# Column copies in larger groups, a table in the order of lanes, and SP clearing the sums: a graph layer on one core

## The chip, the cores and the metric

The kernel runs on one core of a Trainium2 chip. The metric is the time of the program on the device in microseconds. Times of runs are given as the median of several; a profile is one execution, taken by the hardware profiler. The core has five engines with instruction queues of their own: TensorE (PE, with its weight loads listed as PEld), VectorE (DVE), ScalarE (ACT), GpSimd (POOL) and SyncE (SP). In the profile a name such as DVEq or SPq stands for the queue's own work: loading registers, waiting, issuing transfers.

## The reference

`x` holds 12500 nodes of 48 numbers; 400000 edges have a source `src`, a destination `dst` (sorted) and 32 attributes. Cut to what matters:

```python
h = maximum(layernorm(x), 0)                      # 12500 x 48
tmp = concatenate([h[dst], h[src], edge_attr], axis=1)   # 400000 x 128
hid = relu(tmp @ W1 + b1)                         # 400000 x 128
msg = hid @ W2 + b2                               # 400000 x 48
x = x + segment_sum(msg, dst, num_segments=12500)
```

## The kernel before

**Tables.** `h @ W1` is not computed per edge. `node_tables` normalizes the nodes and writes two tables to HBM, with 128 numbers for each node: `tab_a` (destination part with the bias) and `tab_b` (source part). The source table is also made a second time on chip, in `bt`, turned: 128 partitions hold the 128 hidden numbers, and each node is one column. `turn(i)` makes 1024 columns of it: four matmuls into PSUM and a copy by ACT (line 307). Node number `p * 98 + r` belongs to lane `p`, and column `n` of `bt` is node `n`, so the copy writes each lane's numbers 98 columns apart. Thirteen turns are spread over the first five iterations, `TURNS = 3` each.

**Chunks.** The main loop in `windows` runs over 391 chunks of 8 tiles of 128 edges (and two more iterations to drain). Its order is written out by hand (`tc.manual_schedule()`); each engine executes its own share in that order. For a chunk `c`:
- SP issues the loads of the edge attributes (`lhs`), of the destination numbers (`row`) and of the 80 rows of `tab_a` at the chunk's window (`rhs`), line 354 to 364. The window's address is a register: line 361 loads it together with the 15 node numbers of this chunk's row transfers.
- DVE makes the one-hot matrix of the window (`lhs`, line 379), and the compared `hot` (line 389).
- PE multiplies both parts (`before`, line 400), adds the source part (`gathered`, line 421), ACT applies the ReLU (`hidden`, line 437), and PE sums over edges by the one-hot matrix (`fold`, line 445, 448) into `p_g`. DVE adds `p_g` to the running sums of the window (`add`, line 460) two iterations later.

**The source part comes three ways.** Of the 8 tiles in a chunk, most are gathered from `tab_b` by POOL, one indirect transfer of 128 rows each (line 371) into one of seven buffers `gb`. About one tile in eight chunks is collected by SP, one transfer per row (`rows`, line 289, 15 per chunk). And about 1.1 tiles per chunk are collected from the turned table `bt` on chip by `columns`: one copy per edge, of one column of 128 numbers, from an address in a register (line 348). `PARTS` lists the groups of these copies: engine (True is DVE), place in the strip of addresses, count. For each group the queue loads its addresses from SBUF into registers (`numbers`, line 272) and then copies. In an iteration DVE has groups of 8, 15, 16, 20 and 12 (71 copies) and ACT groups of 12, 8, 8, 20, 12 and 12 (72 copies), 143 together; a load takes a whole number of fours, and in the group of 15 the 16th register is the place of the sum (`PLACE`).

**Segments.** Sums are kept for 1024 nodes at a time in one of two buffers `segs`, for 12 chunks (`GQ`), `k` counting them. At `k = 11` `segment_next` clears the other buffer by two memsets on DVE (line 476) and carries 80 columns over. In the next segment PE multiplies the old sums by `W2` at `k = 0` and `1` (`segment_sum`, line 488, 489), DVE adds the result to `x` (`segment_add`, line 495), and at `k = 2` SP stores it (line 499).

An `If` on a flag chooses between `windows` and a general path, which doesn't run with these inputs.

Of the kernel before, what the change touches and what calls it, by code (L numbers as in the profile page):

```python
# [8 lines left out]
F32 = mybir.dt.float32  # L9
# [42 lines left out]
TURNS = 3  # L52
BLOCKS = (NPAD + CE - 1) // CE
BUILD = (BLOCKS + TURNS - 1) // TURNS
COLS = BUILD
# [10 lines left out]
STRIP = 144  # L66
# [3 lines left out]
RPART = 15  # L70
BASE = 0

BT0 = 16512
SEG0 = 161696
# [3 lines left out]
AT_PLACE, AT_SEG, SEG, NEXT = 16, 17, 18, 19  # L78
WIDTH = 20
# [13 lines left out]
EPS = 1e-5  # L93

# [135 lines left out]
def windows(nc, tc, gp, bt, ident, idx, raw, rhss, x_t, tab_a, tab_b, dst, edge_t, w2s, b2s,  # L230
            sources, out_t):
# [4 lines left out]
    with ExitStack() as es:  # L236
# [24 lines left out]
        gss = {}  # L261

# [31 lines left out]
        bt_v = bt.rearrange("h (p r) -> h r p", r=NR)  # L294

        def turn(i):

            n = min(T, NR - i * T)
            p_t = ps_p.tile([P, T, HID], F32, name="pre")
            parts = p_t.rearrange("h (k q) p -> h k q p", k=2)  # L300
            for k in range(2):
                nc.tensor.matmul(
                    parts[:, k, : n // 2, :].rearrange("h q p -> h (q p)"), wb[:, k, :],
                    ht[: 2 * D, i * T // 2 : (i * T + n) // 2, :].rearrange("k g p -> k (g p)"),
                    start=True, stop=True,
                )
            nc.scalar.copy(
                bt_v[:, i * T : i * T + n, :].rearrange("h (q k) p -> h q k p", k=2),
                parts[:, :, : n // 2, :].rearrange("h k q p -> h q k p"),
            )  # L310
# [14 lines left out]
        def columns(c, part):  # L325

            dve, at, n = PARTS[part]
            first = (c - COLS) * PART + FIRST_OF[part]
            n = max(0, min(n, len(BYCOLS) * P - first)) if c >= COLS else 0
            engine = mybir.EngineType.DVE if dve else mybir.EngineType.Activation  # L330
            copy = nc.vector.tensor_copy if dve else nc.scalar.copy
            place = PLACE if at < PLACE <= at + PARTS[part][2] and c >= 2 else None
            size = -(-n // 4) * 4 if place is None else place + 1 - at
            if not n:
                if place is not None:
                    st[c - 2]["base"], = numbers(c, place, 1, engine, cols)
                return
            got = numbers(c, at, size, engine, cols)
            if place is not None:
                st[c - 2]["base"] = got[place - at]  # L340
            for k, of in enumerate(got[:n]):
                j, e = divmod(first + k, P)
                if j not in gts:
                    gts[j] = gtc.tile([HID, P], F32, name="gt")
                of = of.with_bounds(
                    min_val=BT0, max_val=BT0 + 4 * (N - 1), guaranteed_mod_val=0, out_of_modulus=4
                ) - BT0
                copy(gts[j][:, e : e + 1], bt8[:, bass.ds(of, 4)].bitcast(F32))  # L348

        def prepare(c):  # L350
# [10 lines left out]
            base, *nodes = numbers(c, BASE, 1 + m, mybir.EngineType.SP)  # L361
# [109 lines left out]
        def segment_next(g):  # L471

            old, new = segs[g % 2], segs[(g + 1) % 2]
            if g > 0:
                for k in range(2):
                    nc.vector.memset(new[:, k, W:], 0.0)  # L476
# [24 lines left out]
        with tc.manual_schedule():  # L501
            for c in range(NCH + 2):
# [9 lines left out]
                columns(c, 1)  # L512
# [35 lines left out]
                for i in range(c * TURNS, min((c + 1) * TURNS, BLOCKS)):  # L548
                    turn(i)
# [130 lines left out]
def tile_gnn_preln(  # L680
# [15 lines left out]
    ones: bass.AP,  # L696
    w1: bass.AP,
# [52 lines left out]
    with tc.tile_pool(name="keep", bufs=1) as keep, tc.tile_pool(  # L750
# [69 lines left out]
        def check():  # L820
# [10 lines left out]
            nc.vector.tensor_scalar(cols, cols, 4, BT0, op0=ALU.mult, op1=ALU.add)  # L831
            rows_at = slice(BASE, BASE + 1 + RPART)
# [7 lines left out]
            at = last[:, :, AT_PLACE : AT_PLACE + 1]  # L840
            nc.vector.scalar_tensor_tensor(
                at, last[:, :, AT_SEG : AT_SEG + 1], -4.0, at, op0=ALU.mult, op1=ALU.add
            )
            at_place = slice(PLACE, PLACE + 1)
            nc.vector.scalar_tensor_tensor(
                cols[:, :, at_place], cols[:, :, at_place], 1.0, at, op0=ALU.mult, op1=ALU.add
            )

# [5 lines left out]
    with tc.If(outside == 0) as cmp:  # L854
        windows(nc, tc, gp, bt, ident, (srci, rel, bw, wrow, last, cols, degs), (xg, wb, ht), rhss,
                x_t, tab_a, tab_b, dst16, edge_t, w2s, b2s, sources, out_t)
# [78 lines left out]
```

## Time and profile before

| | us |
|---|---|
| median of 3 runs (lowest, highest) | 3365.4 (3362.7, 3370.7) |
| the profiled execution | 3372.65 |
| its span | 3370.8 |
| DVE, ACT, POOL, PE busy | 2800, 3036, 2530, 2776 |

A row of grouped instructions reads: line, engine, operation, output <- inputs, shapes, count | busy time in us, mean of one in ns | idle time of the engine just before them, and what ended most of it. Copies are pipelined, so the mean of one (144 ns on DVE) is longer than their pace. "issue" is idle time in which the engine waited for nothing that the profile shows. In a timeline a row gives start and duration in us, and neighbouring instructions of one kind are merged (x15). A row of waits gives who waited, for whom, total us, times, longest.

### The profile page before, as it was taken

Reading aid. Unit: us, or ns where it says so; the run is one execution under the profiler, and the core shown is the slowest. Engines: PE = TensorE matmul, PEld = TensorE weight load, DVE = VectorE, ACT = ScalarE, POOL = GpSimd, SP = SyncE. Lnnn points to the kernel's source line nnn. Section 1 sums busy time; section 2 is a strip of 40 time slices with the busy share of each in tenths; the row PEclk is TensorE's granted clock in tenths of the full one; section 3 lists DMA queues with packets and bytes.
Section 4 is the critical chain, followed back from the end, with each engine's and each line's share of the span. In section 5 each row is a group of like instructions: output and inputs, shape, how many; then the busy total and the mean of one; then the engine's idle time right before and its main releaser. Section 6 shows DMA issues by size and latency. Waiting matters only on the chain.

```text
span 3370.8 us, 115212 instructions
## 1 busy us (share of the span) xinstructions
PE 2775.6 (82%) x16394; PEld 2158.3 (64%) x16394; DVE 2800.1 (83%) x29140; ACT 3035.6 (90%) x28179; POOL 2530.0 (75%) x2670
## 2 busy tenths in 40 slices
PE   7987778888888888888887788888788788788777
PEld 6666666666666666666666666676666666666565
DVE  6588888888888888888888888888888888888876
ACT  5799998999998999998899999889998999999987
POOL 7677777777777777777777777777777777777776
PEclk9999998998898998988889999888998999899989
DMA  7433333333333333333333333333333333333333
GB/s 262 122 97 104 100 97 100 99 101 100 100 99 100 95 100 102 100 101 97 100 98 101 100 100 102 95 101 97 102 99 98 97 100 98 104 100 97 99 96 83
DMA packets 200234, 349.24 MB, mean 104 GB/s; under 512 B 69219, under 2 KB 107749, under 8 KB 198181
## 3 DMA queue, kind: packets, MB, share of 16 engines
q0 software_dynamic: 84800, 172.53, 18.9%
q1 hardware_dynamic: 114258, 169.09, 16.7%
q14 instruction: 634, 5.19, 0.5%
q8 instruction: 138, 2.26, 0.3%
q10 hardware_dynamic: 404, 0.17, 0.0%
HBM read 322.05 MB, written 22.07 MB: 102 GB/s over the span
## 4 chain that ended last, share of the span: by engine, by line
DVE 71%; issue 14%; PE 5%; DVEq 4%; POOL 2%; DMA 2%; ACT 0%; SPq 0%; POOLq 0%; ACTq 0%
DVE gt L348 47%; DVE lhs L379 12%; DVE hot L389 8%; DVEq L272 4%; DVE seg L460 2%; POOL gb L371 2%; PE pre L400 1%; PE p_g L445 1%; DVE xseg L495 1%; DVE seg L476 1%; DMA row<-in_dst 1%; PE p_f L488 1%; PE p_f L489 1%; DMA gb<-tab_b,srci 1%; PE p_n L195 1%
## 5 line engine op out<-in xcount | busy, mean ns | idle before, releaser
L371 POOL DMA_INDIRECT gb<-tab_b,srci x2618 | 2489.4, 951 | 812.7 <-issue 724.4
L348 ACT COPY gt<-bt 128x1 f32 x27705 | 2618.0, 188 | 63.9 <-issue 54.6
L348 DVE COPY gt<-bt 128x1 f32 x27335 | 1842.1, 144 | 463.3 <-issue 435.1
L400 PEld LDWEIGHTS pre<-rhs,lhs 112*128 112x128 f32 x6250 | 823.5, 208 | 277.1 <-issue 193.4
L400 PE MATMUL pre<-rhs,lhs 112*128 112x128 f32 x6250 | 841.5, 292 | 98.3 <-issue 56.7
L445 PE MATMUL p_g<-hot,hid 128*128 128x80 f32 x6250 | 794.0, 282 | 131.2 <-ACT hid L437 129.1
L445 PEld LDWEIGHTS p_g<-hot,hid 128*128 128x128 f32 x6250 | 758.4, 198 | 164.4 <-ACT hid L437 161.6
L421 PE MATMUL pre<-gb,ident 128*128 128x512 f32 (+2 forms) x1548 | 771.2, 627 | 34.3 <-DMA gb<-tab_b,srci 26.5
L437 ACT ACTIVATE hid<-pre 128x1024 f32<-128x1024 f32 x391 | 397.5, 1017 | 220.2 <-PE pre L421 205.8
L379 DVE TENSOR_SCALAR_CACHE_REDUCE lhs<-row,bw 80x1024 f32<-80x1024 int16 x391 | 494.6, 1265 | 14.8 <-DMA row<-in_dst 14.5
L421 PEld LDWEIGHTS pre<-gb,ident 128*128 128x128 f32 x1548 | 311.8, 225 | 281.0 <-issue 261.7
L421 PE MATMUL pre<-ident,gt 128*128 128x128 f32 x860 | 214.9, 336 | 261.7 <-DVE gt L348 234.7
L421 PEld LDWEIGHTS pre<-ident,gt 128*128 128x128 f32 x860 | 143.8, 210 | 291.5 <-issue 136.4
L389 DVE TENSOR_TENSOR hot<-wnum,rel 128x640 f32<-128x640 f32 x391 | 318.2, 814 | 0.0
L460 DVE TENSOR_TENSOR seg<-seg,p_g 128x160 f32 x391 | 121.5, 311 | 47.8 <-PE p_g L448 47.8
L448 PE MATMUL p_g<-ident,deg 80*128 80x80 f32 x782 | 156.4, 283 | 0.0
L448 PEld LDWEIGHTS p_g<-ident,deg 80*128 80x128 f32 x782 | 123.6, 198 | 0.0
L488 PE MATMUL p_f<-seg,w2s 128*48 128x512 f32 (+1 forms) x134 | 82.2, 700 | 44.3 <-DVE xseg L495 43.9
L489 PE MATMUL p_f<-seg,b2s 1*48 1x512 f32 (+1 forms) x134 | 76.2, 650 | 0.0
L488 PEld LDWEIGHTS p_f<-seg,w2s 128*48 128x48 f32 x134 | 12.3, 135 | 85.9 <-DVE xseg L495 60.0
L476 DVE MEMSET seg<- 128x944 f32 x64 | 54.1, 845 | 9.3
L489 PEld LDWEIGHTS p_f<-seg,b2s 1*48 1x48 f32 x134 | 11.3, 122 | 65.2 <-issue 65.2
(76 smaller groups left out, 429.0 us busy)
## 6 DMA issues: line engine op xcount, KB each, us to landing
gs<-tab_b SPq DMA_DIRECT2D x5760, 0.5 KB
row<-in_dst SPq DMA_DIRECT2D x390, 160.0 KB
lhs<-in_edge_t SPq DMA_DIRECT2D x390, 128.0 KB
gb<-tab_b,srci POOLq DMA_INDIRECT x2618
rhs<-tab_a SPq DMA_DIRECT2D x391, 40.0 KB
xseg<-in_x_t SPq DMA_DIRECT2D x33, 192.0 KB
out_x<-xseg SPq DMA_DIRECT2D x33, 192.0 KB
tab_b<-tab SPq DMA_DIRECT2D x3, 1280.0 KB
```

Of the source, the lines that this page charges most:

```text
L272: return nc.values_load_multi_w_load_instructions(table[c % P : c % P + 1, c // P, at : at + n], engines=[engine], min_val=0, max_val=1 << 23,
L348: copy(gts[j][:, e : e + 1], bt8[:, bass.ds(of, 4)].bitcast(F32))
L371: nc.gpsimd.indirect_dma_start(out=gb[:, t, :], out_offset=None, in_=tab_b[:, :], in_offset=bass.IndirectOffsetOnAxis(ap=srci[:, c * T + t ...
L379: nc.vector.tensor_scalar(lhs[:W, : n * P], row[:, : n * P], bw[:, c : c + 1], None, op0=ALU.is_equal, op1=ALU.add, accum_out=deg[:, :1],)
L389: nc.vector.tensor_tensor(hot[:, :n, :], wnum.unsqueeze(1).to_broadcast([P, n, W]), rel[:, c * T : c * T + n].unsqueeze(2).to_broadcast([P ...
L400: nc.tensor.matmul(pre[:, t, :], s["lhs"][:K, t * P : (t + 1) * P], s["rhs"][:K, :], start=t % BANK == 0, stop=False, skip_group_check=True,)
L421: nc.tensor.matmul(pre[:, t:e, :], lhsT, rhs, start=False, stop=True, skip_group_check=True)
L437: nc.scalar.activation(h[:, :n, :], s["pre"][:, :n, :], AF.Relu)
L445: nc.tensor.matmul(p_g[:, 0, :], s["h"][:, t, :], s["hot"][:, t, :], start=t == 0, stop=t == n - 1)
L448: nc.tensor.matmul(p_g[:, 1, :], s["deg"], ident[:W, :W], start=True, stop=True)
L460: nc.vector.tensor_add(to, to, s["p_g"])
L488: nc.tensor.matmul(p_f[:, :n], w2s, seg[:, 0, s], start=True, stop=False)
```

## The change

- `bt` is written in the order of lanes: node `p * 98 + r` becomes column `r * 128 + p`, so a turn's copy writes runs of 128 columns. The 13 turns go to six iterations, as 2, 2, 2, 2, 3, 2, and the column copies begin at chunk 6 instead of 5.
- The addresses of columns are worked out on chip from node numbers, by a few more passes of DVE over the strips before the loop.
- 148 columns per chunk instead of 143: DVE in groups of 23, 16, 17, 16 (with the sum's place as the 24th register of the first), ACT in groups of 12, 16, 20, 12, 16. Two of ACT's groups stand before the activation and three behind it, as 28 and 44 copies before and 28 and 48 after.
- 16 rows per chunk by SP instead of 15; SP loads the node numbers of two chunks at once (32 registers), and the windows' addresses of eight chunks at once.
- The memsets of a segment's sums go; SP writes zeros from HBM over them in eight pieces, one per iteration from `k = 2` to `9` of the following segment.

```diff
-TURNS = 3
...
+TURNS = (2, 2, 2, 2, 3, 2)
+COLS = len(TURNS)
...
 PARTS = (
-    (True, 0, 8), (True, 8, 15), (True, 24, 16), (True, 40, 20), (True, 60, 12),
-    (False, 72, 12), (False, 84, 8), (False, 92, 8), (False, 100, 20), (False, 120, 12),
-    (False, 132, 12),
+    (True, 0, 23), (True, 24, 16), (True, 40, 17), (True, 60, 16),
+    (False, 76, 12), (False, 88, 16), (False, 104, 20), (False, 124, 12), (False, 136, 16),
 )
...
-RPART = 15
-BASE = 0
+RPART = 16
+BASE, BASES = 2 * RPART, 8
+CLEAR = 8
...
             nc.scalar.copy(
-                bt_v[:, i * T : i * T + n, :].rearrange("h (q k) p -> h q k p", k=2),
+                bt[:, i * CE : i * CE + n * P].rearrange("h (q k p) -> h q k p", k=2, p=P),
                 parts[:, :, : n // 2, :].rearrange("h k q p -> h q k p"),
             )
...
-            base, *nodes = numbers(c, BASE, 1 + m, mybir.EngineType.SP)
+            if c % BASES == 0:
+                bases[:] = numbers(c, BASE, BASES, mybir.EngineType.SP)
+            if c % 2 == 0 and c + 1 >= ROWS0:
+                ahead[:] = numbers(c, 0, 2 * RPART, mybir.EngineType.SP)
+            base, nodes = bases[c % BASES], ahead[c % 2 * RPART :][:m]
...
         def segment_next(g):
             old, new = segs[g % 2], segs[(g + 1) % 2]
-            if g > 0:
-                for k in range(2):
-                    nc.vector.memset(new[:, k, W:], 0.0)
...
+        def segment_clear(g, k):
+
+            n = 2 * (L - W) // CLEAR
+            half, at = divmod(k, CLEAR // 2)
+            nc.sync.dma_start(
+                segs[g % 2][:, half, W + at * n : W + (at + 1) * n],
+                zeros.unsqueeze(0).to_broadcast([P, n]),
+            )
...
                 columns(c, 0)
-                columns(c, 1)
                 segment_add()
                 if 0 <= c - 2 < NCH:
                     add(c - 2)
                     if k == GQ - 1:
                         segment_next(g)
-                columns(c, 2)
+                columns(c, 1)
                 if c < NCH:
                     compare(c)
...
+                columns(c, 2)
                 columns(c, 3)
                 columns(c, 4)
                 columns(c, 5)
-                columns(c, 6)
-                columns(c, 7)
                 if 0 <= c - 1 < NCH:
                     gathered(c - 1)
                     hidden(c - 1)
+                columns(c, 6)
+                columns(c, 7)
                 columns(c, 8)
-                columns(c, 9)
-                columns(c, 10)
...
+                if g > 0 and begin(g + 1) < NCH and 0 <= k - STORE < CLEAR:
+                    segment_clear(g - 1, k - STORE)
...
+            nc.vector.tensor_scalar(
+                at, cols, 1.0 / NR, 0.5 / NR - 0.5, op0=ALU.mult, op1=ALU.add
+            )
+            nc.vector.tensor_scalar_add(at, at, ROUND)
+
+            nc.vector.tensor_scalar(
+                at, at, -ROUND, 4.0 - 4.0 * NR * P, op0=ALU.add, op1=ALU.mult
+            )
+            nc.vector.tensor_scalar_add(at, at, float(BT0))
+
             nc.vector.scalar_tensor_tensor(
-                cols[:, :, at_place], cols[:, :, at_place], 1.0, at, op0=ALU.mult, op1=ALU.add
-            )
+                cols, cols, 4.0 * P, at, op0=ALU.mult, op1=ALU.add
+            )
```

More of the change, by code (lines that the diff above doesn't have):

```diff
@@ L93 @@
 EPS = 1e-5
+ROUND = 1.5 * 2**23
 G = 5
@@ L261, in windows @@
         gss = {}
+        bases, ahead = [], []
         def group(c):
@@ L547, in windows @@
                     sources()
-                for i in range(c * TURNS, min((c + 1) * TURNS, BLOCKS)):
-                    turn(i)
+                if c < COLS:
+                    for i in range(sum(TURNS[:c]), sum(TURNS[: c + 1])):
+                        turn(i)
                 if c < PIECES:
@@ L696, in tile_gnn_preln @@
     ones: bass.AP,
+    zeros: bass.AP,
     w1: bass.AP,
@@ L883 @@
     numbers[2 : NCH + 2, AT_PLACE] = SEG0 + of % 2 * SEG_SIZE - BT0
-    numbers[:NCH, BASE] = first
+    bases = np.pad(first, (0, -NCH % BASES)).reshape(-1, BASES)
+    numbers[: len(bases) * BASES : BASES, BASE : BASE + BASES] = bases
     numbers[:NCH, SEG] = seg
```

38 lines of the change are left out of this document (20 added, 18 removed).

## The prediction

> **What bounds the kernel now.** I read the page first (shares, chain), then the timeline of one engine over one iteration, then the waits of each engine between 130 and 3340 us, where 383 of the 391 chunks run.
>
> ```profile
> span 3370.8 us, 115212 instructions
> PE 2775.6 (82%) x16394; PEld 2158.3 (64%) x16394; DVE 2800.1 (83%) x29140; ACT 3035.6 (90%) x28179; POOL 2530.0 (75%) x2670
> ...
> DVE 71%; issue 14%; PE 5%; DVEq 4%; POOL 2%; DMA 2%; ACT 0%; SPq 0%; POOLq 0%; ACTq 0%
> ...
> L371 POOL DMA_INDIRECT gb<-tab_b,srci x2618 | 2489.4, 951 | 812.7 <-issue 724.4
> ```
>
> ACT has the highest busy share, yet the chain that ended last is DVE's, with 14% "issue": DVE waiting for nothing that the profile shows. The timeline of DVE in one iteration says what this is:
>
> ```profile
> 1509.83 1.28 DVE L379 TENSOR_SCALAR_CACHE_REDUCE lhs<-row,bw 80x1024 f32<-80x1024 int16 x1
> ...
> 1511.04 0.57 DVE L348 COPY gt<-bt 128x1 f32 x8
> 1512.02 1.00 DVE L348 COPY gt<-bt 128x1 f32 x15 [0.42 <-issue]
> 1512.94 0.31 DVE L460 TENSOR_TENSOR seg<-seg,p_g 128x160 f32 x1
> 1513.78 1.06 DVE L348 COPY gt<-bt 128x1 f32 x16 [0.52 <-issue]
> 1514.76 0.81 DVE L389 TENSOR_TENSOR hot<-wnum,rel 128x640 f32<-128x640 f32 x1
> 1515.76 1.30 DVE L348 COPY gt<-bt 128x1 f32 x20 [0.19 <-issue]
> 1517.30 0.82 DVE L348 COPY gt<-bt 128x1 f32 x12 [0.24 <-issue]
> 1518.04 1.26 DVE L379 TENSOR_SCALAR_CACHE_REDUCE lhs<-row,bw 80x1024 f32<-80x1024 int16 x1
> ```
>
> A gap stands before nearly every group of copies, where DVE's queue is loading the group's addresses into registers (line 272). One load of each size, from the view of that line in windows that hold one load (8, 12, 16, 20 registers), and the 31 loads of a single register:
>
> ```profile
> L272 DVEq TENSOR_LOAD <-cols x1: 607/607/607, 1501.7 to 1501.7; - x1
> ...
> L272 DVEq TENSOR_LOAD <-cols x1: 853/853/853, 1508.1 to 1508.1; - x1
> ...
> L272 DVEq TENSOR_LOAD <-cols x1: 1107/1107/1107, 1504.3 to 1504.3; - x1
> ...
> L272 DVEq TENSOR_LOAD <-cols x1: 1351/1351/1351, 1506.0 to 1506.0; - x1
> ...
> L272 DVEq TENSOR_LOAD <-last x31: 303/314/545, 224.9 to 3239.6; - x31
> ```
>
> (1351 - 607) / 12 = 62 ns per register, and 607 - 8 x 62 = 111 ns beside them. The five loads (8, 16, 16, 20, 12) take 607 + 2 x 1107 + 1351 + 853 = 5025 ns of an iteration of 1518.04 - 1509.83 = 8.21 us; the other 3.2 us hand out 71 copies and a few large operations, at most 43 ns each. So it is DVE's queue, not its datapath, that is full. It hardly waits for others:
>
> ```profile
> DVE gt L348 <- issue: 432.8, 1267, 1.2
> DVE seg L460 <- PE p_g L448: 21.0, 10, 3.4
> ...
> 130.00:3340.00 3210.00, 2644.51 (x15768) 2061.72 (x15767) 2717.82 (x28896) 2954.66 (x27991) 2429.21 (x2556) 0.91 0.36 99
> ```
>
> The rows are the waits and the window's busy times (PE, PEld, DVE, ACT, POOL). 21 us in 3210 is all that PE costs DVE. POOL is as full: 951 + 724.4 us / 2374 gaps = 1.256 us per gather, and 2618 of them are 3288 us. What it waits for, and its one long stall:
>
> ```profile
> POOL gb L371 <- PE pre L421: 16.4, 50, 1.5
> ...
> 127.82 0.95 POOL L371 DMA_INDIRECT gb<-tab_b,srci  x1 [12.98 <-PE pre L421]
> ```
>
> So DVE's queue and POOL run at nearly the same pace, and neither can gain much alone.
>
> **The change, part by part.**
>
> *DVE's groups.* With 148 column copies per chunk from chunk 6, there are (390-6) x 148 / 128 = 444 column tiles (430 before) and 48 row tiles (45). DVE does 72 copies per iteration for 71, in groups of 23, 16, 17, 16 for 8, 15, 16, 20, 12. Loads go up to whole fours, and the first takes the sum's place along: 24, 16, 20, 16 registers for 8, 16, 16, 20, 12. What differs is one load of 24 for one of 8 and one of 12: 111 + 24 x 62 = 1599 ns for 607 + 853 = 1460, **+139 ns** in 384 iterations: **+53 us**. No row has a load of 24; the line through four rows is taken, as the row of 20 is nearest to it. The ends are -20 us (if all of the single register's 303 ns were fixed cost, 303 - 111 = 192 ns more fall away with the load: -53 ns) and +98 us (if 24 cost what 8 and 16 do, 1714 ns: +254 ns). The 72nd copy costs at most 43 ns of the queue, and one load fewer to turn to gives about as much back: 0, ends -17 and +17 us. The datapath's part, 72 x 61 ns, lies under the queue.
>
> Here a page speaks the other way. The Trainium skill, page "DMA: Bandwidth & Descriptors", section "Latency and other measured facts", puts a floor of about 600 ns under a tensor load. By that, one load fewer would take up to 0.6 us off each iteration, 230 us in all, and POOL would set the end. The rows of one register (303 ns) contradict it here; the case it makes stands among the rivals.
>
> *Sums cleared by SP, not DVE.* At a segment's end DVE cleared 2 x 944 columns:
>
> ```profile
> 1526.28 1.27 DVE L379 TENSOR_SCALAR_CACHE_REDUCE lhs<-row,bw 80x1024 f32<-80x1024 int16 x1
> ...
> 1529.05 0.31 DVE L460 TENSOR_TENSOR seg<-seg,p_g 128x160 f32 x1
> 1529.51 1.84 DVE L476 MEMSET seg<- 128x944 f32 x2
> ...
> 1532.32 0.81 DVE L389 TENSOR_TENSOR hot<-wnum,rel 128x640 f32<-128x640 f32 x1
> ...
> 1535.53 1.27 DVE L379 TENSOR_SCALAR_CACHE_REDUCE lhs<-row,bw 80x1024 f32<-80x1024 int16 x1
> ```
>
> From sum to compare it is 3.27 us here and 1.82 us in the iteration above, but this iteration is only 9.25 - 8.24 = 1.0 us longer than the one before it, as the loads run under the clearing; 0.31 us of that (load of one register) and the 0.18 us copy stay. So 0.5 us x 31 = **-16 us**, not the 57 us that the memsets are busy; ends 0 (work only leaves DVE) and -45 (1.45 us x 31). DVE's waits for p_g come from the segment sums on PE, which stay, but PE gets more time per iteration: **-8 us** of 21 (ends 0, -21).
>
> *SP.* Its queue does about one iteration in 7.5 us:
>
> ```profile
> 1534.46 0.33 SPq L354 DMA_DIRECT2D lhs<-in_edge_t  x1
> ...
> 1537.03 4.81 SPq L289 DMA_DIRECT2D gs<-tab_b  x15
> 1541.95 0.33 SPq L354 DMA_DIRECT2D lhs<-in_edge_t  x1
> ...
> SPq L499 <- DVE seg L460: 153.4, 24, 12.0
> SPq L499 <- DVE xseg L495: 50.7, 8, 9.2
> ...
> L272 SPq TENSOR_LOAD <-last x449: 274/1187/1317, 134.7 to 3331.4; - x150
> ...
> 8.94 0.46 SPq L770 DMA_DIRECT2D last<-in_src_last  x1
> 9.44 0.93 SPq L771 DMA_DIRECT2D cols<-in_src_strip  x1
> ```
>
> One load of 32 registers per two chunks, at (1187 - 274) / 15 = 61 ns each, is 2.17 us for 2 x 1.19, and eight bases every eight chunks take 0.70 us back: nothing in sum, but even chunks come 1 us later and odd ones earlier. The 16th row DMA adds 4.81 / 15 = 0.32 us. The 256 clearing DMAs (8 x 32 segments) go to 128 partitions, as the last two rows do: 0.46 us taken, end 0.93. Per segment that is 12 x 0.32 + 8 x 0.46 = 7.5 us, against the 204 / 32 = 6.4 us that SP now stands waiting at the store (line 499). Queued behind each clearing DMA are the next chunk's edges, indices and window rows, for which DVE's compare and PE wait. The first of them waits for PE's last sum over that segment, which is done by then: the store just ahead of it has waited for DVE to add that sum. DVE writes to the cleared segment two iterations after the last piece is issued, so it finds it landed. SP's spare time is used up, and a little shows: **+6 us**, ends 0 and +39 (0.32 x 391 + 0.46 x 256 - 204).
>
> *ACT.*
>
> ```profile
> L348 ACT COPY gt<-bt 128x1 f32 x27608 | 2608.8, 188 | 63.3 <-issue 54.0 <-ACT gt L348 1.0
> L437 ACT ACTIVATE hid<-pre 128x1024 f32<-128x1024 f32 x383 | 389.7, 1017 | 192.1 <-PE pre L421 190.8 <-ACT gt L348 0.3
> ```
>
> (Both rows are of the window, not the page.) ACT's copies go from 72 to 76 per iteration, 1479 more at 94.5 ns (2608.8 us / 27608), +140 us, in groups of 12, 16 before the activation and 20, 12, 16 behind it. They fit into 192 + 63 us of idle time: 0, end +20 (no gain is possible, as work is only added).
>
> *POOL.* 2601 gathers for 2618: -17 x 1.256 = -21 us of its own time, all of it turned into waiting, as DVE is slower: 0.
>
> *Start.* Four iterations have two turns where they had three, and the last two have three and two in place of one and none; the node numbers' conversion adds four passes over 608 columns to DVE.
>
> ```profile
> L307 ACT COPY bt<-pre 128x1024 f32<-128x1024 f32 (+1 forms) x13 | 25.0, 1988 | 3.5 <-PE pre L302 3.5
> ...
> 44.11 0.45 DVE L831 TENSOR_SCALAR cols<-cols 128x576 int32<-128x576 int32 x1
> ```
>
> A turn's copy wrote with steps of 98 numbers; in the order of lanes it writes runs of 128, as `hid` does in 1017 ns (above): 13 x 0.97 = 12.6 us less on ACT. Columns start one iteration later, and the conversion costs 4 x 0.45 = 1.8 us. **+1 us**, ends -12 and +12.
>
> Sum: 53 + 0 - 16 - 8 + 6 + 0 + 0 + 1 = **+36 us**. The profiled run took 3372.65 us (span 3370.8, the rest around it), 7 us over the median of the three runs, 3365.4; against that median, 3365 + 36 = **3401 us**, +1.1%.
>
> **The rivals.**
> - *POOL decides, the load is mostly fixed cost* (faster). If a load of 24 takes no longer than those of 8 and 12 together (1460 ns), DVE's time falls by 16 + 8 us and more, and the end follows POOL: 3365 - 21 to 3365 - 21 - 16 (its waits for PE), about **3340**. For it: POOL's 1.256 us cadence hardly breaks. Against: the four loads lie on one line, 246, 254 and 244 ns per four registers.
> - *SP falls behind* (slower still). It decides once a clearing DMA's issue costs over 0.46 us: halfway to 0.93 it is 0.23 x 256 = 59 us on top of SP's +39: up to 3463; about **3440**. For it: spare 6.4 against 7.5 us per segment. Against: a slower DVE gives SP time too.
> - *ACT becomes the bound.* 76 x 94.5 + 1017 = 8.2 us per iteration, under 8.3; only if waits for PE stay as they are, 3365 + 140 - 63 = **3442**. In the Trainium skill, page "Perfetto Trace Analysis", section "Identifying the Most-Contended Engine", the engine of highest occupancy is the bound, which here is ACT, and adding to it would cost the full 140 us: 3505. Its 190.8 us of waits for PE say that it is not.
> - *Nothing comes of it*: the load's increase and what DVE loses cancel (53 - 45 - 8 = 0): **3365**.
>
> **How the numbers follow.** Sum as forecast (3375 to 3425) 0.55; SP 0.15; ACT 0.08; POOL 0.15; nothing 0.07. What a measurement of this kernel can tell from no change is about 0.2%, 7 us. So faster 0.15, same 0.07, slower 0.78. From half of POOL's case to most of SP's: 3345 to 3445.
>
> **What the changed profile would show.** The load of 24 near 1.6 us in DVE's queue, four loads per iteration, iterations near 8.35 us; POOL's waits for PE grown from 16 to some 70 us; ACT's waits for `pre` down to about 80 us; SP's waits at the store near zero, and no more than a few us of DVE waiting for `row`. The prediction is wrong if the load of 24 takes under 1.46 us, if POOL still runs without waits at a shorter total, or if DVE waits for `row` by tens of us.

## The result: 7% slower, and SP late

The changed kernel takes 3606.7 us (median of four runs, 3603.6 to 3614.2) against 3367.3 us for the kernel before beside it: a ratio of 1.0715 (95% interval 1.0692 to 1.0739). The forecast was 3401 us. The sign was right; some 205 us are missing from the sum. The profiled execution took 3609.8 us.

The page of the changed kernel: span, busy shares, the chain that ended last by engine, and two groups of instructions.

```profile
span 3608.0 us, 117497 instructions
...
PE 2891.0 (80%) x16428; PEld 2244.8 (62%) x16428; DVE 2782.5 (77%) x29394; ACT 3222.8 (89%) x29658; POOL 2494.4 (69%) x2653
...
DVE 27%; SPq 24%; DMA 15%; PE 14%; issue 11%; ACT 5%; DVEq 2%; POOL 1%; ACTq 0%; POOLq 0%
...
L373 POOL DMA_INDIRECT gb<-tab_b,srci x2601 | 2454.0, 943 | 1036.5 <-issue 733.5
...
L381 DVE TENSOR_SCALAR_CACHE_REDUCE lhs<-row,bw 80x1024 f32<-80x1024 int16 x391 | 495.8, 1268 | 117.4 <-DMA row<-in_dst 115.3
```

DVE's share of the chain fell from 71% to 27%. In its place stand SP's queue (24%) and transfers (15%), neither of which was over 2% before. All engines lost busy share. So much of the chain now waits for what SP issues. (ACT is still the busiest, at 89%, and has 5% of the chain. The Trainium skill, page "Perfetto Trace Analysis", section "Identifying the Most-Contended Engine", would name it as the bound; this chain does not.)

The waits of the engines, between 130 and 3580 us of the changed kernel:

```profile
POOL gb L373 <- PE pre L423: 259.0, 134, 7.5
...
ACT hid L439 <- PE pre L423: 168.8, 114, 6.3
...
DVE lhs L381 <- DMA row<-in_dst: 102.0, 126, 2.2
...
DVE seg L462 <- PE p_g L450: 18.8, 11, 2.9
```

One row of the same view of the kernel before, for comparison with the third:

```profile
DVE lhs L379 <- DMA row<-in_dst: 2.1, 5, 0.9
```

SP's queue in the changed kernel, same window. Line 289 issues the 16 row transfers; line 507 is the store at a segment's end:

```profile
SPq L289 <- DMA seg<-in_zeros: 58.8, 89, 1.7
SPq L289 <- DMA lhs<-in_edge_t: 57.7, 102, 1.5
SPq L507 <- DVE seg L462: 46.4, 23, 6.1
SPq L289 <- DMA row<-in_dst: 35.9, 102, 1.6
SPq L507 <- DVE xseg L503: 9.3, 7, 2.0
```

And before:

```profile
SPq L289 <- DMA row<-in_dst: 2.5, 7, 0.5
...
SPq L289 <- DMA lhs<-in_edge_t: 1.0, 4, 0.5
```

Two things are to be seen. First, SP itself is held up: its row transfers wait 152 us (58.8 + 57.7 + 35.9) for earlier transfers to land, where they waited 3.5 us for `lhs` and `row` before. The operands in the trace say how: each of SP's transfers signals one of eight semaphores in turn, and first waits until the transfer eight places earlier, which had the same one, has landed. (In the timeline below, the clear at 2013.82 us and the row at 2018.30 both have semaphore 102; that row starts 1.35 us after the row ahead of it, where 0.32 us is usual.) Second, `row` is late for DVE in 126 chunks, and yet SP still stands 56 us at the store.

The register loads came out as forecast. One load each of 24, 16 and 20 registers, from windows that hold one load:

```profile
L272 DVEq TENSOR_LOAD <-cols x1: 1598/1598/1598, 1529.6 to 1529.6; - x1
...
L272 DVEq TENSOR_LOAD <-cols x1: 1096/1096/1096, 1553.7 to 1553.7; - x1
...
L272 DVEq TENSOR_LOAD <-cols x1: 1351/1351/1351, 1551.7 to 1551.7; - x1
```

SP's timeline over one segment of the changed kernel shows what a clear does to it:

```profile
2004.63 0.37 SPq L485 DMA_DIRECT2D seg<-in_zeros  x1
2005.09 0.38 SPq L352 DMA_DIRECT2D lhs<-in_edge_t  x1
...
2008.64 5.13 SPq L289 DMA_DIRECT2D gs<-tab_b  x16
2013.82 0.36 SPq L485 DMA_DIRECT2D seg<-in_zeros  x1
2014.29 0.36 SPq L352 DMA_DIRECT2D lhs<-in_edge_t  x1
...
2015.95 6.44 SPq L289 DMA_DIRECT2D gs<-tab_b  x16
2022.45 0.36 SPq L485 DMA_DIRECT2D seg<-in_zeros  x1
2022.92 0.37 SPq L352 DMA_DIRECT2D lhs<-in_edge_t  x1
...
2069.57 0.33 SPq L352 DMA_DIRECT2D lhs<-in_edge_t  x1
...
2085.67 0.33 SPq L352 DMA_DIRECT2D lhs<-in_edge_t  x1
...
2096.47 5.16 SPq L289 DMA_DIRECT2D gs<-tab_b  x16
2104.41 0.34 SPq L507 DMA_DIRECT2D out_x<-xseg  x1
```

Two chunks with clears take 2022.92 - 2005.09 = 17.8 us of SP; two without take 2085.67 - 2069.57 = 16.1 us. Of the 1.7 us, 0.9 us are the two issues (2004.63 to 2005.09: 0.46 us each). The rest is mostly waiting: the 16 rows take 5.13 us in the chunk where a register load stands between `row` and `rhs`, and 6.44 us in the next one, where nothing does and the rows come round to the clear's semaphore before it has landed. At the end SP is done with its rows at 2101.63 and stands 2.8 us until the store can go.

### The profile page after: what moved, and what is told of

It is laid out like the page before. It is cut to its first block, busy times and chain, and to the rows that moved or that the text cites. A ratio compares the mean times of both kernels' runs of the same rounds, so it can differ in the third digit from the quotient of the medians.

```text
span 3608.0 us, 117497 instructions
## 1 busy us (share of the span) xinstructions
PE 2891.0 (80%) x16428; PEld 2244.8 (62%) x16428; DVE 2782.5 (77%) x29394; ACT 3222.8 (89%) x29658; POOL 2494.4 (69%) x2653
## 4 chain that ended last, share of the span: by engine, by line
DVE 27%; SPq 24%; DMA 15%; PE 14%; issue 11%; ACT 5%; DVEq 2%; POOL 1%; ACTq 0%; POOLq 0%
DVE gt L346 17%; SPq L289 13%; DMA row<-in_dst 11%; DVE lhs L381 5%; SPq L272 5%; PE pre L402 4%; ACT gt L346 4%; PE pre L423 4%; DMA rhs<-tab_a 3%; DVE hot L391 3%; PE p_g L447 2%; SPq L352 2%; DVEq L272 2%; SPq L485 2%; SPq L354 1%
## 5 line engine op out<-in xcount | busy, mean ns | idle before, releaser
L373 POOL DMA_INDIRECT gb<-tab_b,srci x2601 | 2454.0, 943 | 1036.5 <-issue 733.5
L346 ACT COPY gt<-bt 128x1 f32 x29184 | 2820.4, 187 | 122.6 <-issue 77.6
L402 PEld LDWEIGHTS pre<-rhs,lhs 112*128 112x128 f32 x6250 | 858.7, 216 | 338.9 <-issue 246.2
L402 PE MATMUL pre<-rhs,lhs 112*128 112x128 f32 x6250 | 880.6, 300 | 141.7 <-DVE lhs L381 113.2
L447 PE MATMUL p_g<-hot,hid 128*128 128x80 f32 x6250 | 811.3, 286 | 133.1 <-ACT hid L439 132.5
L447 PEld LDWEIGHTS p_g<-hot,hid 128*128 128x128 f32 x6250 | 778.5, 203 | 162.0 <-ACT hid L439 160.7
L423 PE MATMUL pre<-gb,ident 128*128 128x512 f32 (+2 forms) x1548 | 799.7, 650 | 0.0
L423 PE MATMUL pre<-ident,gt 128*128 128x128 f32 x888 | 234.3, 353 | 382.1 <-DVE gt L346 338.8
L423 PEld LDWEIGHTS pre<-gb,ident 128*128 128x128 f32 x1548 | 328.7, 235 | 254.2 <-issue 234.8
L503 DVE TENSOR_TENSOR xseg<-xseg,p_f 48x512 f32<-48x512 f32 (+1 forms) x67 | 44.6, 666 | 9.5 <-PE p_f L497 9.5
```

Source lines behind the costliest of these rows:

```text
L373: nc.gpsimd.indirect_dma_start(out=gb[:, t, :], out_offset=None, in_=tab_b[:, :], in_offset=bass.IndirectOffsetOnAxis(ap=srci[:, c * T + t ...
L402: nc.tensor.matmul(pre[:, t, :], s["lhs"][:K, t * P : (t + 1) * P], s["rhs"][:K, :], start=t % BANK == 0, stop=False, skip_group_check=True,)
L423: nc.tensor.matmul(pre[:, t:e, :], lhsT, rhs, start=False, stop=True, skip_group_check=True)
L447: nc.tensor.matmul(p_g[:, 0, :], s["h"][:, t, :], s["hot"][:, t, :], start=t == 0, stop=t == n - 1)
```

## Experiments

Theory S: SP's queue sets the pace of the changed kernel, since the clears cost it more than their issue. Its rival, theory D: DVE's queue does, with its larger loads. All ratios are to the kernel before.

**1. Which part costs.** Four kernels, each with one part undone or done alone. The changed kernel with the memsets back on DVE and no clears:

```diff
 (segment_next)
+            if g > 0:
+                for k in range(2):
+                    nc.vector.memset(new[:, k, W:], 0.0)
 (loop)
-                if g > 0 and begin(g + 1) < NCH and 0 <= k - STORE < CLEAR:
-                    segment_clear(g - 1, k - STORE)
```

> The changed kernel with the clearing given back to DVE (the two memsets of line 476 of before) and no clearing transfers on SP; everything else stays changed. Theory S (SP's queue sets the time since each clearing transfer costs it about 1 us, its 0.47 us of issue and as much again of waiting for its own earlier transfers): the time falls to what DVE's queue allows, 3410 to 3450 us, and DVE's waits for row go from 115 us to under 10. Theory D (DVE's queue sets it, with the loads of 24 registers and the groups costing far more than the 139 ns forecast; SP's lateness is only a symptom): it stays at 3590 us or above, as the memsets come on top. A third, that SP's 16th row and its loads of 32 are to blame and not the clearing: it stays above 3550.

Measured: 3441.4 us, 1.0218 (1.0201 to 1.0235). That is inside theory S's range. The clears, net of the memsets that they save, cost 3607 - 3441 = 165 us. The larger part of the loss is theirs. DVE's waits for `row` are gone, and POOL's waits for PE fall from 259 us to 65 us. The granted clock of TensorE does not explain the difference: it is 0.886 here, 0.879 in the changed kernel and 0.911 in the kernel before.

The changed kernel with SP's loads per chunk, as before:

```diff
-            if c % BASES == 0:
-                bases[:] = numbers(c, BASE, BASES, mybir.EngineType.SP)
-            if c % 2 == 0 and c + 1 >= ROWS0:
-                ahead[:] = numbers(c, 0, 2 * RPART, mybir.EngineType.SP)
-            base, nodes = bases[c % BASES], ahead[c % 2 * RPART :][:m]
+            base, *nodes = numbers(c, 0, 1 + m, mybir.EngineType.SP)
```

> The changed kernel with SP loading its registers chunk by chunk again (one load of 17: the window's address and 16 nodes) in place of 32 per two chunks and 8 addresses per eight; clearing by SP stays. Theory S in its strict form (a clearing transfer costs SP 1 us whatever else it does): 3590 to 3620 us. Its variant (the waiting comes about because odd chunks have no load between row and the row transfers any more, so that SP runs into its own transfers of eight issues before): SP spends 1.25 us per chunk loading but waits less, 3480 to 3560 us. Theory D: 3607, no change.

Measured: 3576.9 us, 1.0619 (1.0601 to 1.0636): 30 us less than the changed kernel, and outside all three ranges. Its SP hardly waits for clears, `lhs` or `row` to land any more (130 to 3340 us):

```profile
SPq L289 <- DMA rhs<-tab_a: 22.5, 59, 1.4
...
SPq L289 <- DMA row<-in_dst: 3.2, 9, 0.6
...
SPq L289 <- DMA lhs<-in_edge_t: 2.5, 4, 0.9
```

With a load of 17 registers in every chunk, the clear has time to land before the rows come round to its semaphore. But the loads take that time themselves (576 us of SP in all, where the changed kernel's take 467), so little is gained.

Table and larger groups alone (no clears, 15 rows, one load of 16 on SP, memsets on DVE):

```diff
-RPART = 16
+RPART = 15
 (and both edits above)
```

> The changed kernel with SP's work as in the kernel before: 15 rows, one load of 16 per chunk, and the memsets back on DVE. What stays is the turned table in the order of lanes and the larger groups of column copies (148 per chunk). Theory S: DVE's queue alone, 53 to 77 us over before (0.14 to 0.2 us per iteration), 3405 to 3445 us. Theory D: most of the loss stays, over 3520 us. If the larger groups cost nothing: 3367 us or less.

Measured: 3432.5 us, 1.0196 (1.0179 to 1.0213), inside theory S's range. The 16th row and the batched loads, by the difference to 3441, cost some 9 us without the clears.

The kernel before with nothing but its memsets replaced by the eight clears:

```diff
-            if g > 0:
-                for k in range(2):
-                    nc.vector.memset(new[:, k, W:], 0.0)
+ (segment_clear and its call, as in the change)
```

> The kernel before with only the clearing changed: SP's eight transfers per segment in place of DVE's memsets. Theory S with 1 us of SP per clearing transfer: SP takes 7.65 + 1.0 = 8.65 us in eight of twelve chunks against DVE's 8.3, so 3400 to 3440 us, and DVE begins to wait for row. If a clearing transfer costs SP only its issue (0.47 us): 3350 to 3370 us, no change or a little faster by the memsets.

Measured: 3454.9 us, 1.0258 (1.0241 to 1.0275), above both ranges. The clears alone make the kernel before 88 us slower, though its SP had 15 rows, smaller loads, and 204 us of waiting at the store to give.

**2. What in a clear costs.** First its place: behind `rhs`, ahead of the rows, so that `lhs` and `row` go first.

```diff
                     prepare(c)
+                    if g > 0 and begin(g + 1) < NCH and 0 <= k - STORE - 1 < CLEAR:
+                        segment_clear(g - 1, k - STORE - 1)
                     rows(c, st[c].pop("rows"))
 ...
-                if g > 0 and begin(g + 1) < NCH and 0 <= k - STORE < CLEAR:
-                    segment_clear(g - 1, k - STORE)
```

> The changed kernel with each clear one place later in SP's queue: behind the next iteration's `lhs`, `row`, register load and `rhs`, ahead of its 16 row DMAs, instead of just ahead of `lhs` and `row`. Same count, same bytes, same issue cost. Theory L (the clear's 118 KB stand ahead of `lhs` and `row`, make them land late, and SP then waits on them and DVE on `row`): most of the clears' cost goes, 3470 to 3530 us, with SP's waits on `lhs` and `row` (58 and 36 us in the changed kernel) and DVE's wait for `row` (115 us) down to a few us. Theory I (each clear costs SP's queue its issue, and SP is the bound whatever the place): 3580 to 3610 us, SP still late for `row`.

Measured: 3547.2 us, 1.0535 (1.0515 to 1.0556), 60 us less than the changed kernel. Between the theories: SP hardly waits for `lhs` any more, but the rows now wait for the clear 158 times in place of 89. Worked out from the semaphores in the traces, `lhs` and `row` land 2.4 and 3.1 us after their issue here (medians), as in the kernel before (2.4 and 3.0); in the changed kernel, where the clear goes first, it is 3.6 and 3.7 us.

```profile
SPq L289 <- DMA seg<-in_zeros: 62.2, 158, 1.0
...
SPq L289 <- DMA rhs<-tab_a: 35.6, 63, 1.4
```

Then two pieces in place of eight:

```diff
-CLEAR = 8
+CLEAR = 2
```

> The changed kernel with the clears in 2 pieces of 472 KB a segment instead of 8 of 118 KB: the same bytes, 192 fewer SP instructions. Theory I (SP's issues and the waits that each clear brings): some 190 times 0.5 to 1.0 us of SP go, 3450 to 3520 us. Theory B (the bytes are what costs, since they hold up what lands behind them): no gain, 3590 to 3640 us, the waits on the clear's landing fewer but longer (several us each).

Measured: 3522.2 us, 1.0458 (1.0441 to 1.0475), 85 us less. The issues saved are 192 x 0.46 = 88 us, so this is about what theory I says, 2 us above the upper end of its range. Each wait on the clear got longer, though there are fewer (SP's rows: 83.3 us in 32 waits).

Both edits joined, two pieces behind `rhs`:

> The changed kernel with the two edits joined that gave 60 and 85 us: two clears of 472 KB a segment, each behind `rhs` and ahead of the row DMAs. If they are two gains (less queue time; no clear ahead of `lhs` and `row`): 3450 to 3480 us. If they are one (fewer or later clears both only let `row` land in time): 3500 to 3530 us. If a piece of 472 KB in front of the row DMAs holds these up, which wait for the transfer eight back: 3530 to 3560 us.

Measured: 3493.8 us, 1.0366 (1.0349 to 1.0383): 113 us less, of 60 + 85. Largely two gains, not one, but short of the expected 3450 to 3480 us.

Small clears: memsets on DVE, and in addition the eight clears, of 4 columns each (2 KB for 118 KB).

```diff
-                segs[g % 2][:, half, W + at * n : W + (at + 1) * n],
-                zeros.unsqueeze(0).to_broadcast([P, n]),
+                segs[g % 2][:, half, W + at * n : W + at * n + 4],
+                zeros[:4].unsqueeze(0).to_broadcast([P, 4]),
```

> The changed kernel with the memsets back on DVE (3441 us), and 8 clears a segment in the place where the changed kernel issues them, each of 128 partitions by 4 columns (2 KB in place of 118 KB); the memsets clear all of the sums as before, so only SP's instructions and the 128 descriptors of each clear are added. Theory I (issue and queue position cost, whatever the bytes): 3530 to 3600 us. Theory B (the 118 KB cost, by what lands behind them): 3445 to 3490 us.

Measured: 3502.6 us, 1.0389 (1.0366 to 1.0412): 61 us more than without them, between the two theories. So issue and bytes both cost. The bytes add 104 us up to the changed kernel, which has no memsets on top; that they seem dearer is a matter of order, as the table below shows: the issue had some spare time to fill first.

15 rows in place of 16, clears as changed (`RPART = 15`):

> The changed kernel with 15 row DMAs an iteration on SP in place of 16 and a load of 30 registers per two iterations in place of 32; clears stay as they are. Theory Q (SP's queue time sets the pace, so 0.32 us an iteration less on SP comes off the iterations that SP holds back): 3490 to 3530 us. Theory L (the clears' landing holds up `lhs` and `row`, however much time SP has): 3570 to 3600 us.

Measured: 3581.9 us, 1.0628 (1.061 to 1.0646): 25 us less than the changed kernel, inside theory L's range. But SP was not given the 0.32 x 391 = 125 us that theory Q counts on. `BASE` is `2 * RPART`, so the load of the eight windows' addresses now begins at the 31st number of its line and not at the 33rd, and the load of nodes has 30 registers and not 32. Both got longer. In the changed kernel a load of 8 and one of 32 take:

```profile
L272 SPq TENSOR_LOAD <-last x1: 735/735/735, 1372.8 to 1372.8; - x1
...
L272 SPq TENSOR_LOAD <-last x1: 2134/2134/2134, 2006.0 to 2006.0; - x1
```

With 15 rows, the load of 8 and one of 30:

```profile
L272 SPq TENSOR_LOAD <-last x1: 1947/1947/1947, 2004.6 to 2004.6; - x1
...
L272 SPq TENSOR_LOAD <-last x1: 2356/2356/2356, 2023.4 to 2023.4; - x1
```

All of SP's register loads take 564 us there against 467 us, 97 us more. So SP's queue was given some 28 us, and 25 us came out: the run does not speak against theory Q, and it cannot tell Q from L. (That a load is dear when its start or its count is no whole number of fours fits these rows, and the 1.41 us of a load of 17, in the run with loads chunk by chunk, beside 1.19 us for 16 in the kernel before; no run varies it alone.)

What joins these runs is SP's pace in the chunks that have clears. Worked out from the starts of `lhs` in each trace: the mean distance in us from one to the next at `k` = 3 to 9, beside DVE's (starts of its comparison), chunks 20 to 380. (The row with two clears has a clear in two of these chunks only.)

| | SP, `k` 3 to 9 | DVE, `k` 3 to 9 | median, us |
|---|---|---|---|
| before | 7.86 | 8.16 | 3367 |
| before, with clears | 8.58 | 8.43 | 3455 |
| table and groups alone | 7.88 | 8.36 | 3432 |
| changed, memsets on DVE | 8.13 | 8.37 | 3441 |
| the same, and small clears | 8.63 | 8.57 | 3503 |
| changed, two clears behind `rhs` | 8.57 | 8.64 | 3494 |
| changed, 15 rows | 8.92 | 8.83 | 3582 |
| changed | 9.09 | 8.98 | 3607 |

With the changed groups and no clears DVE takes 8.36 us. In every run in which SP takes longer than that, DVE follows SP to within 0.15 us. From 8.13 to 8.63 it is 0.50 us a chunk for issuing a clear, of which the first 0.23 us, up to DVE's 8.36, cost nothing; from 8.63 to 9.09 it is another 0.46 us for its bytes. By DVE's own pace the changed kernel loses (8.98 - 8.37) x 7 chunks x 32 segments = 137 us of the 165 us in these chunks. Most of the rest, 22 us, lies in the chunk of the store (9.86 us against 9.18).

Why the spare did not help is in the other chunks of the same trace. SP's waiting at the store is not a reserve for the chunks behind it: the store waits for DVE, so it takes SP's lead away once a segment, and the clears follow right behind it, at `k` = 2 to 9. In the changed kernel SP takes 8.0 us a chunk at `k` = 10 to 1 where DVE takes 8.8, and so gains 3.3 us; in the chunk of the store it takes 12.4 us against DVE's 9.9 and loses 2.6 of them. That moving the store or the clears elsewhere in the segment would mend this is argued, not tried.

Last, the clears from ACT's queue:

```diff
 (segment_clear)
-            nc.sync.dma_start(
+            nc.scalar.dma_start(
```

> The changed kernel with the 8 clears a segment issued by ACT's queue in place of SP's, at the same point of the order. Theory S (SP's queue is the bound of the changed kernel): SP gets its time back, the memsets stay off DVE, so the time is that of the run with the memsets on DVE (3441 us) or up to 30 us less, 3410 to 3445 us. Theory A (ACT's own queue is full: 89% busy): 256 issues of 0.1 to 0.5 us on ACT delay the hidden layer, 3460 to 3560 us. Theory B (the bytes): `lhs` and `row` still land late, over 3560 us.

Measured: 5166.5 us, 1.5353 (1.5323 to 1.5383), far beyond what any of the three theories meant, though the kernel before took 3368 us beside it. Waits of all engines:

```profile
PEld p_g L447 <- ACT hid L439: 1990.1, 236, 20.2
...
POOL gb L373 <- PE pre L423: 1796.8, 177, 18.9
ACT gt L346 <- issue: 1688.3, 502, 17.8
```

ACT's datapath idles 1688 us behind its own queue, with up to 17.8 us at a time, and the issue of a clear is only 0.34 us long. The operands in the trace show what its queue stands at (start in us, engine, operation, semaphores):

```
2023.42  ACT  copy (the last before the clear)
2037.55  SP   gs<-tab_b        waits for and signals semaphore 106
2038.74  ACT  wait             semaphore 106
2038.79  ACT  seg<-in_zeros    signals semaphore 106
```

ACT's clear takes its place in the same rotation of eight as SP's transfers. It waits until SP has issued the rows ahead of it in the program's order and the one with the same semaphore has landed; ACT, which was 15 us ahead, stands still that long, and everything behind it.

**3. DVE's groups against ACT's copies.** 65 us of the loss are there without any clear (3432 against 3367). The kernel before with its first two groups made one:

```diff
-    (True, 0, 8), (True, 8, 15), (True, 24, 16), (True, 40, 20), (True, 60, 12),
+    (True, 0, 23), (True, 24, 16), (True, 40, 20), (True, 60, 12),
```

> The kernel before with one edit: its first two groups of copies on DVE, 8 and 15 with the place, are one group of 23 with the place, so four register loads of 72 registers instead of five of 72; copies, ACT's groups, table, SP as before. Theory D (DVE's queue sets the iteration, 0.117 us for each load beside 62 ns for each register): 0.11 us an iteration less, some 40 us, 3320 to 3335 us. Rival P (POOL's gathers stand just behind DVE and take over): 3340 to 3355 us. Rival C (a load of 24 cannot be prefetched past the comparison of `lhs`, and its whole 1.64 us stands in the open where 0.6 did): no gain or a loss, 3365 to 3400 us.

Measured: 3362.2 us, 0.9987 (0.9977 to 0.9997): the only version below the kernel before, by too little to matter. Theory D's 40 us did not come. The chain, and POOL's gathers (groups by line):

```profile
DVE 45%; issue 15%; POOL 15%; PE 10%; ACT 7%; DMA 4%; DVEq 3%; SPq 1%; ACTq 1%; POOLq 0%
...
L371 POOL DMA_INDIRECT gb<-tab_b,srci x2618 | 2481.0, 948 | 814.2 <-issue 751.6 <-PE pre L421 34.8 <-DMA gb<-tab_b,srci 15.9
```

948 ns and 751.6 us / 2464 gaps = 305 ns are 1.253 us a gather, 3280 us for all 2618, and beside them POOL waits only 51 us for others (75 us in the kernel before). So POOL was all but full already: it had 75 us to give, and gave 24. That 3362 us is its floor at 143 copies and 15 rows, above the 3340 to 3355 us that rival P gave it, is argued from this row: in the chain DVE fell from 71% to 45%, and POOL rose from 2% to 15% only.

Table and larger groups alone, with ACT's last group cut from 16 to 12 (ACT 72 copies, DVE's loads 76 registers), and the same run with DVE's groups as 23, 16, 20, 12 (DVE's loads 72 registers, ACT 76 copies):

```diff
-    (False, 76, 12), (False, 88, 16), (False, 104, 20), (False, 124, 12), (False, 136, 16),
+    (False, 76, 12), (False, 88, 16), (False, 104, 20), (False, 124, 12), (False, 136, 12),
```

> The run with the table and the larger groups alone (3432 us: no clears, 15 row DMAs and a load of 16 on SP, memsets on DVE), with ACT's last group cut from 16 copies to 12: ACT 72 an iteration as before, DVE 72 in its four groups as changed; 4 copies an iteration go back to POOL (some 12 gathers, 15 us of POOL's floor). Theory D (DVE's groups are what the 66 us of that run are): 3425 to 3440 us, unchanged. Theory A (ACT's 76 copies and the hidden layer fill its iteration, 7.0 + 1.0 us and the idle between loads, and set the pace): 3365 to 3395 us.

```diff
-    (True, 0, 23), (True, 24, 16), (True, 40, 17), (True, 60, 16),
+    (True, 0, 23), (True, 24, 16), (True, 40, 20), (True, 60, 12),
```

> The same run with DVE's groups 23, 16, 20, 12 in place of 23, 16, 17, 16: 71 copies and four loads of 72 registers where 72 copies took four loads of 80; ACT 76 as changed. 8 registers less at 62 ns and a copy less are 0.53 us an iteration of DVE's queue. Theory D: the time falls to where POOL's floor or ACT holds it, 3345 to 3390 us. Theory A (ACT's 76 copies set the pace): 3415 to 3435 us, and the hidden layer waits for PE no more than in that run.

Measured: 3422.4 us, 1.016 (1.0137 to 1.0182), and 3407.2 us, 1.011 (1.0091 to 1.013). The first is 3 us below theory D's range, the second between the two ranges. (The second expectation counts 80 registers before; groups of 23, 16, 17 and 16 take loads of 24, 16, 20 and 16, which are 76, so the saving is some 0.29 us an iteration and not 0.53.) Neither goes back to 3367: each engine has a floor of its own above it, and the chains say whose it is. ACT 72:

```profile
DVE 73%; issue 15%; PE 5%; DVEq 4%; ACT 3%; DMA 0%; ACTq 0%; SPq 0%
```

DVE 71:

```profile
ACT 64%; DVE 11%; PE 10%; issue 6%; ACTq 4%; POOL 3%; DMA 1%; DVEq 1%; SPq 1%; POOLq 0%
...
L346 ACT COPY gt<-bt 128x1 f32 x29184 | 2819.2, 188 | 100.2 <-issue 60.5
```

So both theories of this pair hold, one under the other: DVE's loads without ACT's 76 copies give 3422 us, ACT's 76 copies without the larger loads 3407, both together 3432. All three have the new table. ACT's floor can be read from the rows: 2819.2 / 391 = 7.2 us of copies, 1.0 us of activation and 100.2 / 391 = 0.26 us of idle time before its groups are 8.5 us an iteration.

A version of the parts that were left (lane order, 71 copies on DVE in loads of 72 registers, ACT 74, 16 rows with one load of 17, memsets on DVE):

> A version made of the parts that the runs leave standing: lane-order table and addresses on chip as changed, 16 row DMAs with one load of 17 registers on SP, no clears, memsets on DVE; DVE 71 copies in four loads of 72 registers, ACT 74. 145 copies and 16 rows an iteration in place of 143 and 15: three pieces, some 9 gathers of 1.25 us, 11 us less on POOL. If POOL's floor holds (the kernel before stood on it): 3345 to 3360 us. If ACT's 74 copies or SP's 16th row set the pace: 3370 to 3420 us.

Measured: 3407.9 us, 1.012 (1.0092 to 1.0148). No gain. Its chain has ACT at 38% and SP's queue at 12%, so ACT's copies and the 16th row, with its load of 17 registers, are the likeliest causes; what each takes was not separated.

Four more kernels ran on a chip on which the kernel before took 5398 us, with DVE and ACT idle although the profile shows nothing that they waited for: the timeline has gaps of 0.5 us and more between copies of one group. That they lacked instructions is a guess; no trace shows the cause. DVE's copies in the first of them, whose idle time is four times that of the same copies elsewhere (479 us in the run with 71 and 76 copies):

```profile
L346 DVE COPY gt<-bt 128x1 f32 x27264 | 2022.5, 145 | 2060.1 <-issue 2028.4 <-ACT bt L305 2.1 <-remote 0.6
```

The table and the merged group alone, and the same with 74 copies on ACT (`(False, 136, 12)` or `14`):

> DVE 71 copies in four loads of 72 registers, ACT 72, 15 row DMAs, no clears, memsets on DVE: of the change only the lane-order table, its addresses on chip and the merged first group are left. Against the kernel before with the merged group (3362 us) it differs by the table alone. If the table costs or gives only at the start: 3350 to 3366 us. If the copies out of it, or the later start of the columns, cost in the loop: 3370 to 3400 us.

> As the run with 71 and 72 copies, with 74 on ACT: two copies an iteration less for POOL, some 6 gathers or 7.5 us of POOL's floor. If ACT fits (74 copies and the hidden layer, some 8.3 us, under POOL's 8.4 us an iteration): 3345 to 3360 us. If ACT's own pace sets the end, as with 76 (3407 us): 3375 to 3410 us.

Measured: 1.0016 (1.0002 to 1.0031) and 1.0111 (1.0095 to 1.0128), at 5406.6 and 5457.6 us. The other two were first runs of the 15 rows and of the two clears behind `rhs`, with the expectations that stand above: 1.0254 (1.0237 to 1.0271) and 1.0273 (1.0252 to 1.0294), at 5536.3 and 5542.0 us. With that much idle time in all of them, the kernel before too, none of these can say what sets the pace elsewhere. What the table's order is worth in the loop stays open for that reason.

## Why the prediction was wrong

- **SP, +6 us (ends 0 and +39): the step that failed.** Measured, the clears cost 165 us in the changed kernel and 88 us in the one before. The issue was as forecast: 0.46 us. Two things were not in the step. It set 7.5 us against 6.4 us over a whole segment, though the spare is at the store and the clears are behind it: chunk by chunk, 7.86 + 0.32 + 0.46 = 8.6 us of SP meet DVE's 8.36 us, already too long by some 0.28 x 7 x 32 = 63 us. (By the one iteration of 7.5 us that the prediction reads, 8.3 us would just have fitted; the mean of these chunks is 7.86.) And it counted only issue; that a slowly landing transfer holds up SP's own next ones through the eight semaphores was not seen (0.46 us more a chunk). Its end of +39 rested on the same average, and for the +6 itself no working is given. SP's waits at the store, forecast near zero, are 56 us: shortage and spare stand in different chunks of one segment.
- **The rival "SP falls behind", 3440 us** was the right mechanism at too low a price: it gave SP up to 39 + 59 = 98 us, and the clears cost 165. Its condition, an issue over 0.46 us, was the wrong one: the issue stayed at 0.46 us, and SP fell behind all the same. The time that a slower DVE gives SP, its counterargument, is what the store takes away.
- **DVE's groups, +53 us: right, as far as it was separated.** The load of 24 took 1598 ns, 1599 were forecast, and with ACT as before and the memsets kept, the run took 3422 us, 55 us more than before (46 to 61 by its interval). The 72nd copy at 0 is within that. The new table is in that run too, and what it is worth in the loop was not measured. The floor of some 600 ns under a load, of the Trainium skill, page "DMA: Bandwidth & Descriptors", section "Latency and other measured facts", would have made this run faster; it was not, and loads of one register took 303 ns.
- **ACT, 0 (end +20): too low, and hidden.** 76 copies give 3407 us on their own, 45 us over the run with the merged group and 72 (whose table is the old one). Beside DVE's loads they add 10 us (3432 against 3422). The fit of 8.2 us into 8.3 us left out the idle time in front of ACT's groups, 0.26 us an iteration.
- **Memsets, -16 us, and the waits for `p_g`, -8 us.** The waits went from 21.0 to 18.8 us, -2. What the memsets give was not separated: no run took them off DVE without giving the clears to another queue.
- **POOL, its gain turned into waiting: right in kind.** Its waits for PE grew to 259 us, not some 70, and ACT's waits for `pre` fell to 169 us, not to 80: most of both is SP's lateness, passed on by DVE and PE. With the memsets on DVE and no clears, POOL's waits for PE are 65 us, near the forecast, and ACT's for `pre` 38 us.
- **Start, +1 us: its parts came out, the sum was not measured.** A turn's copy takes 963 ns, 1.0 us less than before (0.97 were forecast), and POOL's long stall is 10.8 us in place of 13.0.
- **The sign to look for** was named: DVE waiting for `row` by tens of us. It waits 102 us.

## What to carry to other kernels

An average of spare time is no reserve. Ask where in the loop it lies and what stands between it and the added work: here the store, which waits for another engine, takes the queue's lead away just ahead of the chunks that need it, and the comparison to make is the queue's own period against the consumer's in those chunks. Cost an added transfer by its issue and by its landing: where the transfers of a queue take turns on a few semaphores, a slow one holds up those that come round to its semaphore, and one that is issued from another engine ties that engine to the queue. And where several engines stand within 2% of each other, relieving one shows only the next floor; each has to be measured with the others relieved. Last, read in the trace what a small edit did: a count of 15 for 16 moved where a register load begins, and gave back most of what it was to save.

## What the runs showed of the hardware that was not expected

- A transfer of 118 KB to 128 partitions costs SP's queue in this order as much by its bytes (0.46 us a chunk, by waiting for landings) as by its issue (0.46 to 0.50 us). Of 2 KB, it still costs 61 us in all.
- A load of 8 registers took 0.73 us when it began at the 33rd number of its line, and 1.95 us when it began at the 31st; a load of 30 took 2.36 us where one of 32 took 2.13 us.
- The same transfers, issued by ACT, made the kernel 1.54 times as long, by the order of the semaphores and not by their issue (0.34 us).
- On one chip the kernel before took 5398 us against 3367 us elsewhere, and in the first kernel profiled there DVE stood 2060 us in front of its copies, for nearly all of it with nothing in the profile to wait for. The cause is open.
